# A transformer block with expert-choice routing on one core: routing's second search by two bits a round, its first list on four engines, an add moved behind a gather, and constants made later

## The chip, the cores and the metric

The kernel runs on one core of a Trainium2 chip. The metric is the device time of one execution in microseconds (us). A core has five engines that run their own instruction streams and meet at semaphores: PE (TensorE, matmuls and transposes), DVE (VectorE), ACT (ScalarE), POOL (GpSimd) and SP (SyncE, which here issues DMAs). A profile's PEld rows are PE's loads of the stationary operand.

## The reference

The input is `x`, 16 sequences of 256 tokens of width 256 (4096 tokens in all), and one condition vector for each sequence. Everything is float32. Cut to what matters:

```python
shift = silu(t) @ W_ada.T + b_ada
h = ln(x, ln1_g, ln1_b) + shift
q, k, v = (h @ Wqkv.T)                 # 16 heads of 64
q, k = ln(q, qn_g, qn_b), ln(k, kn_g, kn_b)
o = softmax(q @ k.T / 8) @ v
x = x + o @ Wout.T
tok = x.reshape(4096, 256)
gate = softmax(tok @ Wgate.T)          # 8 experts
vals, idx = top_k(gate.T, 512)         # each expert picks its 512 best tokens
g = ln(tok[idx], mlp_g, mlp_b)
y = (gelu(g @ fc1.T + b1) @ fc2.T + b2) * vals
tok[idx] += y                          # scatter-add of all experts
```

## The kernel before

**Attention.** The 16 sequences follow each other, and neighbours overlap. For each sequence the kernel normalises x, projects it in six groups of 512 columns (q, k and v, L611), normalises q and k by head (square on ACT L624, sum on DVE L628, power on POOL L82, scale on DVE L644), transposes them, and takes the heads in quads: scores (L686), row maxima on DVE (L693), exponentials on ACT (L702), normalisation on POOL (L713), transposes on PE (L722), the product with v (L740). The output projection (L764) gives the tokens. They are written to `out`, and, normalised, to a table `xn_dram` that the experts gather from.

**Head.** Before the first projection the kernel loads x of sequence 0, the projection's weights and small tables, and takes the head mean out of the q and k weights ("centering", L531 to L533, eight times). POOL also makes the constants of routing there: block and triangle masks, lane numbers, tile numbers (L85 to L131).

**Routing.** Each of the 8 experts chooses 512 tokens in two halves of 256: the first 256 from the tokens of the first 15 sequences, the second 256 from all tokens that are left. For each half the gates stand as 128 rows of 256 (16 rows for each expert), and a binary search over the 30 bits of a float32 gate finds the value that 256 tokens reach. A round compares all gates with a candidate on DVE (`compare`, L881, with a count for each row), sums the 16 rows of each expert by a matmul on PE (first search `count_over` L911 and L912, second `count` L888), and takes or drops the bit on DVE (`decide` L927, or `drop` and `step`, L893 and L900). Then masks, running sums and offsets give each chosen token its place from 1 to 256 (`masks`, `totals`, `place`), PE turns the places so that tokens lie on partitions (`turn_places`, L967), and `split` makes two numbers of each place: the chunk of 128 and the place in it.

**Jobs.** There are 16 jobs, one for each half and expert. A job needs a list of its token numbers and weights. DVE builds a one-hot of the place for each of 30 or 32 token tiles (`onehot`, L1031) and the values to send there, masked by chunk (`gives`, L1013 and L1021), and PE adds up 30 or 32 small matmuls (`list_matmul`, L1040). `take` reads token numbers and weights from the sum, `gather` fetches the rows by two indirect DMAs on POOL's queue (L1059), PE transposes them (L1068), and two matrix products with GELU between follow (`up` L1087, `gelu` L1094, `down` L1103). `finish` adds the bias and multiplies by the weight on DVE (L1109, L1110), and `scatter` adds the 128 rows to `out` by an indirect DMA on POOL's queue (L1113). Each add waits until the add before it has landed, as both write `out`.

**What sets the order.** Nothing is scheduled by a program at run time: each engine executes its instructions in the order in which the code emits them. Up to job 0 the order comes from a hand-written table: every step has a number (`SEARCH`, `PLACE`, `LIST`, `UP`, `DOWN` and so on), all steps are sorted by it, and emitted. Steps of sequence b in the middle are shifted by `b * PERIOD`. In the table the one-hots of job 0's tiles 25 to 29 stand ahead of tiles 10 to 14; both fives are on POOL, the other twenty on DVE.

From job 1 on a loop emits 16 slots for each job: eight with two matmul pairs of `up`, eight with two of `down`. Into the slots it puts the steps of the second routing, one entry a slot (`second_routing`), the list of the next job (slot 5; in job 7, slot 7), its transposes (slot 14), and the one-hots of the job after it (slots 7 to 15 and 0 to 4). A round of the second search took three slots for the first nineteen bits and two for the last eleven:

```python
new = [partial(b.compare, 29)]
for n in range(29, -1, -1):
    yield from (new, [])
    if n > 10:
        yield []
    new = [partial(f, n) for f in (b.count, b.drop, b.step)]
    new.append(partial(b.compare, n - 1) if n else b.masks)
```

## Time and profile before

| | |
|---|---|
| Median of 3 runs | 1195.77 us (1191.63 to 1196.15) |
| The profiled execution | 1194.45 us, of which the span from first to last instruction is 1192.6 us |
| Mean granted clock of PE | 0.992 |
| Busy share of the span | PE 98%, PEld 69%, DVE 64%, ACT 52%, POOL 50% |
| First matmul, first projection | 5.08 us, 9.02 us |
| First search, first to last count on PE | 867.9 to 909.1 us |
| First list's matmuls | 920.1 to 923.7 us |
| Job 2's gathered rows are transposed | from 963.77 us |
| Second search, first to last count | 958.3 to 1038.7 us |
| Last matmul starts | 1182.4 us |

A line of the timeline gives the start and the length in us, the engine, the line of the kernel, the operation, what it writes and reads, the shapes, how many equal instructions were merged, and in brackets how long the engine was idle before it and what ended that. A letter q after an engine means its queue, issuing a DMA. A line of the waits names who waited for what, the total in us, how often, and the longest. The table by stretches gives for each stretch of time the busy time of each engine.

### The profile page before, as it was taken

Reading aid. Unit: us, or ns where it says so; the run is one execution under the profiler, and the core shown is the slowest. Engines: PE = TensorE matmul, PEld = TensorE weight load, DVE = VectorE, ACT = ScalarE, POOL = GpSimd, SP = SyncE. Lnnn points to the kernel's source line nnn. Section 1 sums busy time; section 2 is a strip of 40 time slices with the busy share of each in tenths; the row PEclk is TensorE's granted clock in tenths of the full one; section 3 lists DMA queues with packets and bytes.
Section 4 is the critical chain, followed back from the end, with each engine's and each line's share of the span. In section 5 each row is a group of like instructions: output and inputs, shape, how many; then the busy total and the mean of one; then the engine's idle time right before and its main releaser. Section 6 shows DMA issues by size and latency. Waiting matters only on the chain. (4 is left out here: it accounts for less than half of the span.)

```text
span 1192.6 us, 19612 instructions
## 1 busy us (share of the span) xinstructions
PE 1162.9 (98%) x6814; PEld 817.1 (69%) x6814; DVE 760.9 (64%) x2274; ACT 624.5 (52%) x1701; POOL 590.7 (50%) x820
## 2 busy tenths in 40 slices
PE   7999999999999999999999999999998989999996
PEld 3566666666676666666666666667755878888885
DVE  7665576666566666666666666565588557865541
ACT  2765655565565656565656566556574422333331
POOL 4665455545555555555554555464674233333332
PEclk9999999999999999999999999999999999999999
DMA  5000000000000000000000000000200446666661
GB/s 187 1 1 5 14 18 19 10 18 10 19 23 5 23 10 19 10 23 6 23 10 28 9 11 14 14 19 19 85 9 1 168 129 186 186 186 185 183 185 22
DMA packets 46738, 62.40 MB, mean 52 GB/s; under 512 B 3888, under 2 KB 39984, under 8 KB 46640
## 3 DMA queue, kind: packets, MB, share of 16 engines
q1 hardware_dynamic: 37680, 49.82, 12.3%
q0 software_dynamic: 6144, 8.39, 3.8%
q10 hardware_dynamic: 2816, 2.95, 0.7%
q8 instruction: 54, 0.88, 0.3%
q14 instruction: 44, 0.36, 0.1%
HBM read 48.56 MB, written 12.58 MB: 51 GB/s over the span
## 5 line engine op out<-in xcount | busy, mean ns | idle before, releaser
L611 PE MATMUL pm<-wq,hT 128*128 128x512 f32 x768 | 365.3, 606 | 2.2 <-ACT qT L665 0.9
L713 POOL TENSOR_SCALAR pr<-pr,sums 128x256 f32<-128x256 f32 x512 | 236.8, 481 | 208.9 <-DVE sums L709 162.2
L82 POOL TENSOR_TENSOR ss<-ss,neghalf 128x8 f32<-128x8 f32 x128 | 211.5, 1653 | 189.8 <-DVE ss L632 185.4
L702 ACT ACTIVATE pr<-sc,nmax 128x256 f32<-128x256 f32 x512 | 236.1, 474 | 116.1 <-DVE nmax L693 111.1
L611 PEld LDWEIGHTS pm<-wq,hT 128*128 128x128 f32 x768 | 134.9, 192 | 126.3 <-issue 112.2
L693 DVE TENSOR_REDUCE nmax<-sc 128x2 f32<-128x512 f32 x256 | 166.5, 683 | 38.3 <-PE sc L686 38.1
L628 DVE TENSOR_REDUCE ss<-sq 128x8 f32<-128x512 f32 x128 | 87.3, 682 | 112.0 <-ACT sq L624 111.5
L722 PEld LDWEIGHTS pp<-ident,pr 128*128 128x128 f32 x1024 | 119.1, 142 | 43.6 <-POOL pr L713 20.3
L722 PE MATMUL pp<-ident,pr 128*128 128x128 f32 x1024 | 139.2, 273 | 0.2
L624 ACT ACTIVATE sq<-pm 128x512 f32<-128x512 f32 x128 | 76.7, 600 | 113.6 <-PE pm L611 107.1
L686 PE MATMUL sc<-kT,qT 64*128 64x256 f32 x1024 | 129.2, 390 | 0.0
L740 PE MATMUL po<-prT,v 128*64 128x256 f32 x1024 | 126.7, 389 | 0.0
L686 PEld LDWEIGHTS sc<-kT,qT 64*128 64x128 f32 x1024 | 93.2, 186 | 40.6 <-issue 30.4
L1103 PE MATMUL py<-w,hid 128*128 128x256 f32 x512 | 118.8, 385 | 0.0
L1087 PE MATMUL ph<-xT,w 128*128 128x256 f32 x512 | 118.4, 384 | 0.0
L764 PE MATMUL pw<-wo,oT 128*128 128x256 f32 x512 | 118.0, 384 | 0.0
L1113 POOL DMA_INDIRECT out<-y,idx x32 | 51.6, 1611 | 123.9 <-DVE y L1110 72.9
L764 PEld LDWEIGHTS pw<-wo,oT 128*128 128x128 f32 x512 | 96.8, 192 | 18.9 <-issue 6.5
L1094 ACT ACTIVATE hid<-ph,vec 128x256 f32<-128x256 f32 x128 | 60.3, 473 | 85.5 <-PE ph L1087 73.4
L1103 PEld LDWEIGHTS py<-w,hid 128*128 128x128 f32 x512 | 95.8, 192 | 13.4
L702 ACT ACTIVATION_READ_ACCUMULATOR pr<-sc,nmax 128x1 f32 x512 | 104.9, 205 | 0.0
L1087 PEld LDWEIGHTS ph<-xT,w 128*128 128x128 f32 x512 | 95.3, 191 | 13.4
(129 smaller groups left out, 1290.7 us busy)
## 6 DMA issues: line engine op xcount, KB each, us to landing
w<-in_fc2T SPq DMA_DIRECT2D x16, 1024.0 KB, 5.6
w<-in_fc1T SPq DMA_DIRECT2D x16, 1024.0 KB, 8.0
out<-tok SPq DMA_DIRECT2D x32, 128.0 KB, 1.7
xn_dram<-tn SPq DMA_DIRECT2D x32, 128.0 KB, 1.7
xs<-in_x SPq DMA_DIRECT2D x15, 256.0 KB, 2.7
b<-in_b2s SPq DMA_DIRECT2D x16, 128.0 KB, 8.2
wq<-in_wqkvT SPq DMA_DIRECT2D x3, 512.0 KB, 6.6
wq<-in_wqkvT ACTq DMA_DIRECT2D x3, 512.0 KB, 6.6
```

Of the source, the lines that this page charges most:

```text
L82: nc.gpsimd.tensor_tensor(dst, src, neghalf[:, : src.shape[1]], ALU.pow)
L611: nc.tensor.matmul(self.pm, hTs[self.b][:, c, bass.ts(self.t, P)], wq[:, c, bass.ts(self.g, GW)], start=(c == 0), stop=(c == DC - 1),)
L628: nc.vector.tensor_reduce(self.ss[:, 0, :], self.sq.rearrange("p (h d) -> p h d", d=HD), AX.X, ALU.add,)
L686: nc.tensor.matmul(self.sc[i, j][:, t, :], qTs[self.b][rows, hp, bass.ts(t, P)], kTs[self.b][rows, hp, :], start=True, stop=True,)
L693: nc.vector.tensor_reduce(self.nmax[i, j], self.sc[i, j], AX.X, ALU.max, negate=True)
L702: nc.scalar.activation(self.pr[i, j][:, t, :], self.sc[i, j][:, t, :], AF.Exp, bias=self.nmax[i, j][:, t : t + 1], scale=1.0, accum_out=se ...
L713: nc.gpsimd.tensor_scalar(self.pr[i, j][:, t, :], self.pr[i, j][:, t, :], self.sums[i][:, 1, j, t : t + 1], 1.0, ALU.mult, ALU.mult,)
L722: nc.tensor.transpose(self.pp[i, j][:, c, bass.ts(t, P)], self.pr[i, j][:, t, bass.ts(c, P)], ident,)
L740: nc.tensor.matmul(self.po[j * HD : (j + 1) * HD, i, :], vs[self.b][:, c, bass.ts(4 * self.d + 2 * i + j, HD)], self.prT[i, j][:, c, :], s ...
L764: nc.tensor.matmul(self.pw, oTs[self.b][:, hp, bass.ts(self.t, P)], wo[:, hp, :], start=(hp == 0), stop=(hp == HP - 1),)
L1087: nc.tensor.matmul(self.ph[f], self.w1[:, c, bass.ts(f, P)], self.xT[:, c, :], start=(c == 0), stop=(c == DC - 1),)
L1103: nc.tensor.matmul(self.py[i], self.hid[:, f, bass.ts(i, P)], self.w2[:, f, :], start=(f == 0), stop=(f == FC - 1),)
```

## The change

- **Constants.** Those of routing leave the head. Six steps placed at `(4 + k/8) * PERIOD` make them in sequence 4. `less` goes; `lane1` (lane numbers from 1), `begin` (−255 in every 16th row, else 0) and the tile numbers times 128 are new. The scaled q gain is made when the first shift is.
- **Head.** The condition is loaded ahead of the vectors. Centering is two operations instead of three. x of sequences 2, 3 and 4 is loaded from ACT's queue, with the output weights, by `last_loads`, behind the first q; before, SP's queue issued them.
- **First search.** The comparison starts its count from `begin`; the second matmul of each round, of one row and one column, goes.
- **Places.** The running sums start from 0 ahead of the offsets; two fused operations add the offset and mask. The turn adds the two kinds of place in PSUM by four matmuls. `split` works on the result in float32.
- **Lists.** `gives` is a product and a difference; for job 0 they run on POOL. The ten one-hots that were on POOL are twenty activations on ACT: `1 - |place - lane|`, clipped at 0. `take` reads the sum in PSUM directly.
- **Second search.** A round tests three candidates and settles two bits: 15 rounds of five slots.
- **Jobs.** `weigh` multiplies the bias by the weight ahead of time, and `finish` is one operation. Job 0's second `scatter` is emitted after the gather of job 2.

`fill` is defined but `FILL` is empty, so it emits nothing. The diff, cut to its core:

```diff
+    def make_vals(k):
+        nc.gpsimd.iota(
+            vals[:, :, :, k], pattern=[[0, E], [P * (1 - k), NT]], base=0, channel_multiplier=k,
+            allow_small_or_imprecise_dtypes=True,
+        )
+    def make_others():
+        nc.gpsimd.memset(gate_of, -1.0)
+        nc.gpsimd.memset(high, 1 << 29)
+        nc.gpsimd.iota(first16, pattern=[[0, 1]], base=0, channel_multiplier=1)
+        nc.vector.tensor_scalar(first16, first16, 15, None, ALU.bitwise_and)
+        nc.vector.tensor_scalar(begin, first16, 0.0, float(1 - CAPL), ALU.is_equal, ALU.mult)
...
+    LOADS = (-61.203, -19.863)
...
-            for g in (1, 3, 5):
+            for g in (5, 1, 3):
                 load_wq(g, nc.scalar)
+        def last_loads():
+            load_x(2, nc.scalar)
             nc.scalar.dma_start(wo, woutT.rearrange("(h p) d -> p h d", p=P))
+            for b in (3, 4):
+                load_x(b, nc.scalar)
...
-            nc.vector.tensor_scalar_mul(ws, ws, 1.0 / HD)
-            nc.vector.tensor_tensor(
-                w3, w3, ws.unsqueeze(2).to_broadcast([P, 8, HD]), ALU.subtract
+            nc.vector.scalar_tensor_tensor(
+                w3, ws.unsqueeze(2).to_broadcast([P, 8, HD]), -1.0 / HD, w3, ALU.mult, ALU.add
...
-                    reach, self.gT, self.cand.bitcast(F32), None, ALU.is_ge, ALU.add,
+                    reach, self.gT, self.cand.bitcast(F32), start, ALU.is_ge, ALU.add,
...
+            def candidates(self, n):
+                self.three = bit.tile([P, 3], I32, tag="three", name="three")
+                for k in range(3):
+                    new = self.three[:, k : k + 1]
+                    if n == 28:
+                        nc.vector.memset(new, (k + 1) << n)
+                    else:
+                        nc.vector.tensor_scalar(
+                            new, self.cand, (k + 1) << n, 0, ALU.bitwise_or, ALU.bitwise_or
+                        )
+            def compare_three(self, n):
+                self.cnt = bit.tile([P, 3], BF16, tag="cnt3", name="cnt3")
+                for k in range(3):
+                    reach = bit.tile([P, 2 * P], BF16, tag="reach", name="reach")
+                    nc.vector.tensor_scalar(
+                        reach, self.gT, self.three[:, k : k + 1].bitcast(F32), None,
+                        ALU.is_ge, ALU.add, accum_out=self.cnt[:, k : k + 1],
+                    )
+            def count_three(self, n):
+                self.pc = ps.tile([P, 3], F32, tag="mm", bufs=3, name="pc")
+                nc.tensor.matmul(self.pc, block, self.cnt, start=True, stop=True)
+            def choose_bits(self, n):
+                enough = bit.tile([P, 3], F32, tag="enough", name="enough")
+                many = bit.tile([P, 1], F32, tag="many", name="many")
+                nc.vector.tensor_scalar(
+                    enough, self.pc, CAPL - 0.5, None, ALU.is_ge, ALU.add, accum_out=many
+                )
+                bits = bit.tile([P, 1], I32, tag="bits", name="bits")
+                nc.vector.tensor_scalar(bits, many, float(1 << n), None, ALU.mult)
+                if n == 28:
+                    self.cand = bits
+                else:
+                    old, self.cand = self.cand, bit.tile([P, 1], I32, tag="cand", name="cand")
+                    nc.vector.tensor_tensor(self.cand, old, bits, ALU.bitwise_or)
...
+                self.compare(n, begin)
...
-                nc.tensor.matmul(self.pc, ones[:1, :P], less, start=True, stop=False)
-                nc.tensor.matmul(self.pc, twice, self.cnt, start=False, stop=True)
+                nc.tensor.matmul(self.pc, twice, self.cnt, start=True, stop=True)
...
-                    offset[:, 1:2], offset[:, 2:3], offset[:, 1:2], ALU.add
...
+            def scans(self):
+                self.place_ = route.tile([P, 2, 2 * P], F32, tag="place", name="place")
                 for m in range(2):
                     nc.vector.tensor_tensor_scan(
-                        place[:, m], ones, self.mask[:, m], offset[:, m : m + 1],
-                        ALU.mult, ALU.add,
-                    )
-                nc.vector.tensor_tensor(place, place, self.mask, ALU.mult)
-                nc.vector.tensor_tensor(place[:, 0], place[:, 0], place[:, 1], ALU.add)
-                self.places = place[:, 0]
+                        self.place_[:, m], ones, self.mask[:, m], 0.0, ALU.mult, ALU.add
+                    )
+            def totals(self):
+                self.po = ps.tile([P, 2], F32, tag="mm", bufs=3, name="po")
+                nc.tensor.matmul(self.po[:, :1], below, self.tot[:, :1], start=True, stop=True)
+                nc.tensor.matmul(self.po[:, 1:], below, self.tot[:, 1:], start=True, stop=False)
+                nc.tensor.matmul(self.po[:, 1:], block, self.tot[:, :1], start=False, stop=True)
+            def place(self):
+                offset = route.tile([P, 2], F32, tag="offset", name="offset")
+                nc.vector.tensor_copy(offset, self.po)
+                for m in range(2):
+                    nc.vector.scalar_tensor_tensor(
+                        self.place_[:, m], self.place_[:, m], offset[:, m : m + 1],
+                        self.mask[:, m], ALU.add, ALU.mult,
+                    )
...
-                    nc.tensor.transpose(
-                        self.pp[:, r, :], self.places[:, bass.ts(r, P)], ident
-                    )
+                    for m in range(2):
+                        nc.tensor.matmul(
+                            self.pp[:, r, :], self.place_[:, m, bass.ts(r, P)], ident,
+                            start=(m == 0), stop=(m == 1),
+                        )
...
+                chunk, place = (
+                    self.part[:, k].rearrange("p (k r) -> p r k", r=2) for k in range(2)
+                )
+                nc.vector.tensor_scalar(chunk, self.pp, P + 0.5, None, ALU.is_gt)
+                nc.vector.scalar_tensor_tensor(
+                    place, chunk, -float(P), self.pp, ALU.mult, ALU.add
+                )
...
-            def gives(self):
+            def gives(self, engine=nc.vector):
                 e, n = self.e, self.tiles
-                chunk = moe.tile([P, NT, KL], BF16, tag="chunk", name="chunk")
-                nc.vector.tensor_tensor(
-                    chunk[:, :n],
+                self.give = moe.tile([P, NT, KL, NV], BF16, tag="give", name="give")
+                engine.tensor_tensor(
+                    self.give[:, :n, 1, :], vals[:, e, :n],
                     self.routing.part[:, 0, e * NT : e * NT + n]
-                    .unsqueeze(2).to_broadcast([P, n, KL]),
-                    lane[:, :KL].unsqueeze(1).to_broadcast([P, n, KL]), ALU.is_equal,
-                )
-                self.give = moe.tile([P, NT, KL, NV], BF16, tag="give", name="give")
-                for c in range(KL):
-                    nc.vector.tensor_tensor(
-                        self.give[:, :n, c, :], vals[:, e, :n],
-                        chunk[:, :n, c : c + 1].to_broadcast([P, n, NV]), ALU.mult,
-                    )
+                    .unsqueeze(2).to_broadcast([P, n, NV]), ALU.mult,
+                )
+                engine.tensor_tensor(
+                    self.give[:, :n, 0, :], vals[:, e, :n], self.give[:, :n, 1, :], ALU.subtract
+                )
...
-                    engine.tensor_scalar(
-                        self.oh[:, t, :], lane, self.routing.part[:, 1, k : k + 1], None,
-                        ALU.is_equal,
-                    )
+                    place = self.routing.part[:, 1, k : k + 1]
+                    if engine is nc.scalar:
+                        off = moe.tile([P, P], BF16, tag="off", name="off")
+                        nc.scalar.activation(off, lane1, AF.Abs, bias=place, scale=-1.0)
+                        nc.scalar.activation(self.oh[:, t, :], off, AF.Relu, bias=1.0, scale=-1.0)
+                    else:
+                        nc.vector.tensor_scalar(
+                            self.oh[:, t, :], lane1, place, None, ALU.is_equal
+                        )
...
+                with nc.allow_low_precision(reason="whole numbers below 2 ** 12"):
+                    nc.vector.tensor_reduce(self.idx, self.pls[:, :, :2], AX.X, ALU.add)
                 self.w = moe.tile([P, KL], F32, tag="w", bufs=4, name="w")
-                nc.vector.tensor_reduce(self.w, ls[:, :, 2:], AX.X, ALU.add)
+                nc.vector.tensor_reduce(self.w, self.pls[:, :, 2:], AX.X, ALU.add)
...
+            def weigh(self):
+                self.bw = moe.tile([P, KL, D], F32, tag="bw", name="bw")
+                for i in range(KL):
+                    nc.vector.tensor_scalar_mul(self.bw[:, i], self.b2, self.w[:, i : i + 1])
             def finish(self, i):
-                nc.vector.tensor_tensor(self.y[:, i], self.py[i], self.b2, ALU.add)
-                nc.vector.tensor_scalar_mul(self.y[:, i], self.y[:, i], self.w[:, i : i + 1])
+                nc.vector.scalar_tensor_tensor(
+                    self.y[:, i], self.py[i], self.w[:, i : i + 1], self.bw[:, i],
+                    ALU.mult, ALU.add,
+                )
...
+        for k, f in enumerate((
+            make_block, make_twice, make_lanes, partial(make_vals, 0), partial(make_vals, 1),
+            make_others,
+        )):
+            at([(4 + k / 8) * PERIOD], f)
...
-            at([p["gives"]], a.gives)
+            at([p["gives"]], partial(a.gives, nc.gpsimd if a is jobs[0] else nc.vector))
...
-                engine = nc.gpsimd if a is jobs[0] and k in (2, 5) else nc.vector
+                engine = nc.scalar if a is jobs[0] and k in (2, 5) else nc.vector
...
-            at(DOWN[i][1:], partial(jobs[0].scatter, i))
+        at([UP[0][0]], jobs[0].weigh)
+        by_end = sorted(range(KL), key=lambda i: DOWN[i])
+        at(DOWN[by_end[0]][1:], partial(jobs[0].scatter, by_end[0]))
...
+            new = [partial(f, 28) for f in (b.candidates, b.compare_three)]
+            for n in range(28, -1, -2):
+                yield from (new, [], [], [], [])
+                new = [partial(f, n) for f in (b.count_three, b.choose_bits)]
+                new += [partial(f, n - 2) for f in (b.candidates, b.compare_three)] if n else [b.masks, b.scans]
...
                     new.list_matmul(0, NT)
                     new.take()
                     new.gather()
+                    if k == 1:
+                        jobs[0].scatter(by_end[1])
...
+                    if s == FC - 1:
+                        a.weigh()
```

## The prediction

> **What bounds the kernel now.** I read the page first, then busy time and granted clock by stretch, the matrix engine's waits, and the timeline of the stretches where it waits.
>
> ```profile
> PE 1162.9 (98%) x6814; PEld 817.1 (69%) x6814; DVE 760.9 (64%) x2274; ACT 624.5 (52%) x1701; POOL 590.7 (50%) x820
> ...
> PE   7999999999999999999999999999998989999996
> ```
>
> PE is busy from end to end: work taken off another engine is worth only what PE waits for it. Counting each PE instruction at its undisturbed spacing in the trace (429 ns for 512 columns, 216 for 256, 109 for a 128-column transpose), I get 1083 us of a 1192.6 us span. Of the rest, about 35 us is spread evenly over the sixteen sequences. What can be moved lies at the head (first matmul at 5.08, then about 11 us lost before 40) and from 875 to 969.
>
> ```profile
> 910.00:914.00 4.00, 3.75 (x21) 1.83 (x19) 3.21 (x10) 0.58 (x1) 0.57 (x2) 0.61 0.01 4
> ...
> 920.00:924.00 4.00, 1.95 (x34) 1.38 (x32) 2.67 (x15) 0.00 (x0) 3.22 (x5) 1.00 0.00 0
> 924.00:928.00 4.00, 4.00 (x12) 3.23 (x11) 3.93 (x25) 0.00 (x0) 2.22 (x2) 0.57 0.21 53
> ...
> 961.00:965.00 4.00, 0.55 (x4) 0.19 (x2) 1.60 (x9) 0.00 (x0) 3.38 (x3) 1.00 0.23 68
> 965.00:969.00 4.00, 4.00 (x13) 3.26 (x14) 0.20 (x1) 1.02 (x2) 0.00 (x0) 0.57 0.30 35
> ```
>
> Columns: length, then busy us of PE, PEld, DVE, ACT, POOL, granted clock, DMA share, GB/s. PE stands still at 920 and 961, and each standstill is paid again: the clock of the next 4 us is 0.57, and there a 256-column matmul takes 0.42 instead of 0.216 us.
>
> ```profile
> PE pc L912 <- DVE reach L881: 4.0, 14, 0.5
> PE px L1068 <- DMA xg<-xn_dram,idx: 3.8, 3, 2.6
> PE pls L1040 <- POOL oh L1031: 1.9, 4, 0.5
> ```
>
> From 850 to 975 these three waits lead: the first search, the gather of job 2, and the one-hots of the first list on POOL.
>
> **1. Second add of job 0 behind a gather: −5.4.**
>
> ```profile
> 949.07 1.67 POOL L1113 DMA_INDIRECT out<-y,idx  x1 [11.43 <-DVE y L1110]
> ...
> 957.61 1.57 POOL L1113 DMA_INDIRECT out<-y,idx  x1 [6.87 <-DMA out<-y,idx]
> ...
> 960.71 1.05 POOL L1059 DMA_INDIRECT xg<-xn_dram,idx  x1
> ...
> 962.06 0.99 POOL L1059 DMA_INDIRECT xg<-xn_dram,idx  x1 [0.30 <-issue]
> ```
>
> The second add waits 6.87 us for the first to land (956.83), and behind it in POOL's queue stand the gates' parts (five operations, 2.0 us) and both gathers of job 2, whose indices have been there since 953.38. PE came for the gathered rows at 961.06 and lost 2.74 + 1.07 us, then about 1.6 to the slow clock. Moved, the gathers are issued at about 953.5 and 954.8. What is late next is their landing: POOL's queue of transfers still holds the first add until 956.83, and the gathers of 934.30 and 935.55, behind weight loads too, took until 939.7 and 940.0. Both give a landing at 957.5 to 959.5, 2 us or more before PE comes. The moved add now waits behind the gathers; who waits for it is only the next job's add, whose y is ready at 960.5. Bounds −3.5 to −6.
>
> **2. First list over four engines: +2.1, a loss.** PE turns the places at 914.65, when DVE had been done since 913.6: the shorter chain before (scans ahead of the totals) is covered by PE. The turn becomes four accumulating float32 matmuls instead of two transposes. A float32 matmul leaves two records (L1103: two of 216 for 256 columns), so 4 × 2 × 109 = 0.87 instead of 0.22 us: +0.65. The split falls from 1.41 (four operations to 916.48) to about 0.88 (two of 0.42 plus gaps), so parts are ready at 916.6, as before. The two "gives" go to POOL: its 128x16 subtraction takes 0.22, the 128x224 one 0.70, so about 0.54 each for 150 columns, 1.1 in all, done by 917.8; PE comes at 920.7, so this is hidden. Gone from POOL are ten one-hots, 6.65 us from 916.57 to 923.22, the wait above. In their place ScalarE does twenty activations of 128 columns, and in its queue they stand behind the last copy of the attention's output:
>
> ```profile
> 916.57 6.65 POOL L1031 TENSOR_SCALAR oh<-lane,partf 128x128 bf16<-128x128 bf16 x10 [6.00 <-DVE partf L981]
> ...
> 917.52 0.58 ACT L750 COPY oT<-po 128x512 f32<-128x512 f32 x1 [2.03 <-PE po L740]
> ```
>
> That copy ends at 918.10, or 918.75 with PE later by 0.65. No 128-column activation is in the trace. The 16-column one lasts 0.21, the 256-column one 0.473 (0.356 from start to start): 0.335 between, the second of each pair reading the first. 20 × 0.335 = 6.7, end 925.45; then 15 list matmuls of 25 ns: PE leaves at 925.85 instead of 923.70. Tiles 25 to 29 are made ahead of 10 to 14, so PE needs the very last. The Trainium skill (ScalarE: Activation LUTs, "Rules for kernel authors") speaks against this step: such cheap functions belong on VectorE, and an activation costs about 0.3 us plus 0.83 ns per element, 0.41 here: by that the twenty take 8.1 us and the loss is 3.6. With half of each pair overlapped (0.335 + 0.24) it is 5.75, loss 1.2. I take the rows. Job 0's gather and VectorE's one-hots of job 1 shift with PE; the slow stretch after it is there already.
>
> **3. First search: −0.6.** Thirty matmuls of 1x1 go. Where PE goes on at once (14 steps) one costs 0.105: −1.5. In the 16 others PE then waits 0.3 to 0.6 for `reach`; the loop of comparison, count and decision (1.05 us) sets the step, and nothing is saved. The comparison gets a second per-partition scalar: the f32 128x256 operation with two (L553, 0.405) lasts 0.05 more than that with one (L1110, 0.353). In 16 waiting steps that is at most +0.9. Bounds −1.5 to 0.
>
> **4. Second search in pairs of bits: +1.3.** PE waited for it nowhere: each count takes 0.03 us of PE and DVE waits for PE (8.8 us, L893). So fewer rounds buy 15 × 0.03 = −0.45, and the second turn of places costs +0.65. DVE pays. Before: 30 × 0.86 (drop 0.19, step 0.20, comparison 0.40 plus its 0.085). Now per round: `enough` with its accumulator 0.25, bits and candidate 0.2 each, three candidates 0.29 (0.15 and two more at 0.065), three comparisons 3 × 0.41 + 0.08: 2.3, × 15 = 34 instead of 26. A job has 16 slots of 0.864 plus list, transposes and counts: 15.1 us. DVE then holds 3.2 rounds 7.4, 30 one-hots at 0.166 5.0, gives 0.6, take 0.3, weighing 0.7, finish 0.9: 14.9. Full, but not over, and lumpy. Worst is job 7's list in slot 5 of job 6: two slots earlier the last choice (0.65), masks (0.9) and now both scans (1.4) run in one piece, then the last three one-hots: 0.2 + 2.95 + 0.5 = 3.65 after the slot began, when PE would be through at 1.73 + 0.75: +1.1. Small waits at two other lists +0.3; job 8's list, which waited 0.28, gains 0.3. Bounds 0 to +6 (rival B).
>
> **5. Head: −1.2.**
>
> ```profile
> 3.40 0.83 POOL L112 IOTA vals<- 128x256 bf16 x1
> 3.71 1.51 DVE L123 TENSOR_SCALAR qgb<-vec 128x2 f32<-128x2 f32 x1 [3.71 <-DMA vec<-in_vecs]
> 3.90 1.33 DVE L543 BATCH_NORM_STATS2 st<-xs 128x6 f32<-128x256 f32 x1
> 4.00 0.94 POOL L116 IOTA vals<- 128x256 bf16 x1
> ```
>
> DVE's two-column operation lasts 1.51 us and ends at 5.22, just as POOL's run of constants ends (5.20); the statistics queued behind it take 1.33 instead of 0.42. Both go: −0.9 on the way to the first projection (9.02), whose weights landed at 7.52. Eight centerings lose an operation of 0.2 us; one is on the path (the scale at 21.21 queues behind it), another less so: −0.3. x of sequences 2 to 4 moves from SP to ScalarE's queue, four issues of 0.4 to 0.7 at about 23 us, where ScalarE is idle for 3.7 us; without that cover it would be 2.0 late. Bounds 0 and −2.5 (the 0.64 clock of 24 to 28 gone too).
>
> **6. Constants in sequence 4: +0.2.** Thirteen POOL operations (4.9 us) at six places. Three fall into idle of 1.7 to 6 us; the others delay POOL by 0.82, 0.66 and 0.65. Normalised scores are ready at least 0.9 us before PE turns them there. VectorE's two operations on `first16` wait for POOL at the last place, with a reciprocal behind them, which POOL itself needs. The skill (SBUF — State Buffer, "SBUF: two separate sides") says that a GpSimd operation and a two-port VectorE one exclude each other; the head's 1.5 us shows such a hold, but only under a run of constants; here each run is under 0.9 us and DVE is busy 64%. By the rule taken at its worst six holds would cost 4 us of DVE, which has it. Bounds 0 and +2.
>
> **7. End: −0.4.** The last finish is one operation instead of two (0.42 + 0.04 + 0.35), and the scatters follow. Of the earlier ones PE waits for none.
>
> Sum: −5.4 + 2.1 − 0.6 + 1.3 − 1.2 + 0.2 − 0.4 = −4.0. The profiled execution took 1194.45 us (span 1192.6): 1190.4. It lies 1.3 below the median of the runs, 1195.77, so I give 1191.8.
>
> **Rivals.**
> A, ScalarE is quick and the head gains in full (20 × 0.29, and the cold clock at 24 gone): list +1.2, head −2.5, search −1.5: −7.2, 1188.6. For it: activations start every 0.356 at 256 columns. Against: the pairs depend. 23%.
> B, slower: VectorE becomes the bound in the second search. If small operations do not overlap (three candidates at 0.19, comparisons at 0.49), a round is 2.7 and a job 16.2 us, over 15.1; it decides from 2.35 us a round. Five jobs × 1.1 in place of small waits: +6 in place of 1.3, so +0.7 in all; with the list at 8.1 us, +2.2: 1198.0. For it: 14.9 of 15.1. Against: candidates overlap now (0.065 apart). 17%.
> C, the reordered gather lands late behind the first add and weight loads, and half of the stall stays: −1.5 instead of −5.4: 1195.7. For it: such a gather took up to 5.4 us to land. Against: 2 us of slack. 18%.
> The sum: 42%.
>
> Within 0.5%, 6 us, is about what a measurement can tell from no change. All of A and a quarter of the likeliest lie below 1189.8: faster 33%. Over 1201.7 only the end of B: 6%. The range reaches from A's far side to near B: 1185.5 to 1197.5; the likeliest case's own is 1189 to 1194.5.
>
> **What would show it.** Right: no wait on job 2's gather and clock 1.0 after it; PE's wait in the first list on ScalarE, not POOL, and longer; first statistics about 0.45 us; job 7's list waits for VectorE. Wrong: PE waiting at most lists of jobs 3 to 7 (B), a first list leaving sooner than before relative to the turn of places (step 2), or sequence 4 longer than its neighbours by over 1 us (step 6).

## The result and the profile after

| | before | after |
|---|---|---|
| Median of 20 runs | 1194.57 us (1191.24 to 1196.17) | 1189.94 us (1187.09 to 1194.47) |
| Ratio of the two | | 0.9968, interval 0.9957 to 0.9979 |
| The profiled execution, its span | 1194.45, 1192.6 us | 1189.26, 1187.5 us |

By the ratio the kernel became about 3.8 us faster (0.32%, interval 0.21 to 0.43%); the medians alone differ by 4.6. The time lies inside the range given and near its likeliest value. The two profiles differ by 5.1 us of span. The sections below show why that is more than the ratio gives, and that the sum came out right with several of its terms wrong.

The page after, busy time and tenths of PE:

```profile
PE 1155.4 (97%) x6783; PEld 814.6 (69%) x6783; DVE 758.9 (64%) x2303; ACT 630.4 (53%) x1721; POOL 585.5 (49%) x813
...
PE   7999999999999999999999999999987999999996
```

PE still bounds the kernel. What PE waits for between 850 and 975 us (line, what it waited for, us in total, times, longest):

```profile
PE pc L956 <- DVE reach L901: 7.1, 16, 0.8
PE pls L1091 <- ACT oh L1081: 3.3, 5, 1.5
PE px L1116 <- DMA xg<-xn_dram,idx: 1.8, 2, 1.3
PE pc L956 <- DVE drop L962: 1.2, 1, 1.2
```

The search's wait has doubled, the first list waits for ScalarE and not POOL, and a wait for gathered rows is still there. But that is another gather: job 1's, at 937, where before only 0.3 us were lost. The stretches (columns as in the prediction: length, busy us of PE, PEld, DVE, ACT, POOL, granted clock, DMA share, GB/s):

```profile
910.00:914.00 4.00, 4.00 (x35) 2.67 (x32) 2.44 (x10) 1.24 (x3) 0.90 (x2) 1.00 0.00 0
916.00:920.00 4.00, 1.45 (x17) 0.93 (x15) 1.86 (x11) 3.78 (x14) 0.00 (x0) 0.96 0.00 0
920.00:924.00 4.00, 3.28 (x23) 2.72 (x24) 2.46 (x16) 0.82 (x3) 1.69 (x2) 0.50 0.03 6
...
940.00:944.00 4.00, 4.00 (x13) 3.18 (x12) 0.00 (x0) 1.02 (x2) 0.00 (x0) 0.57 0.00 0
961.00:965.00 4.00, 4.00 (x23) 3.45 (x22) 3.59 (x23) 1.02 (x2) 1.36 (x1) 1.00 0.32 35
```

The standstill at 961 and the slow clock after it are gone. New are the standstill at 916 to 920, where ACT is busy all the time, and slow stretches at 920 and 940. At 910, where before had a clock of 0.61, the clock is now full, though nothing in the change asks for that. POOL's queue after (start, length, what ended the idle time before):

```profile
950.29 1.67 POOL L1168 DMA_INDIRECT out<-y,idx  x1 [14.30 <-DVE gates L844]
...
954.61 1.03 POOL L1107 DMA_INDIRECT xg<-xn_dram,idx  x1 [0.54 <-DVE idx L1100]
955.94 0.96 POOL L1107 DMA_INDIRECT xg<-xn_dram,idx  x1 [0.30 <-issue]
958.92 1.63 POOL L1168 DMA_INDIRECT out<-y,idx  x1 [2.03 <-DMA out<-y,idx]
...
971.21 1.55 POOL L1168 DMA_INDIRECT out<-y,idx  x1 [5.95 <-DVE give L1068]
973.07 1.01 POOL L1107 DMA_INDIRECT xg<-xn_dram,idx  x1 [0.30 <-DVE reach L922]
```

The gathers of job 2 now stand ahead of the second add of job 0 (958.92). At 971.21 the second add of job 1 still stands ahead of the gather of job 3 (973.07): the same pattern, one job later.

To see where the profiles part, I take the start of the same PE work in both (before, after, difference):

| PE starts | before | after | difference |
|---|---|---|---|
| first projection | 9.02 | 8.45 | −0.56 |
| projection of sequence 1 | 46.35 | 43.51 | −2.84 |
| projections of sequences 2 to 15 | | | −2.84 or −2.85 each |
| first count, last count of the first search | 867.86, 909.07 | 864.93, 907.00 | −2.93, −2.07 |
| first list, first and last matmul | 920.10, 923.67 | 916.51, 921.33 | −3.60, −2.34 |
| transposes of job 1 | 939.73 | 938.68 | −1.05 |
| list of job 2 | 952.08 | 953.24 | +1.16 |
| transposes of job 3 | 982.24 | 977.61 | −4.63 |
| list of job 7, last matmul | 1036.87 | 1032.05 | −4.83 |
| transposes of job 9 | 1075.79 | 1071.11 | −4.68 |
| last matmul; span | 1182.39; 1192.65 | 1177.72; 1187.54 | −4.68; −5.11 |

Read alone, this says: head −2.8 (−2.9 by the first count), search +0.9, first list and what follows +1.0 (places −1.5, list +1.3, slow clock and the rest +1.3), job 1's gather and the slow clock behind it +2.2, job 2's gather −5.8, second search 0, end −0.4. Two of these, the head and the places, are mostly not the change's doing, as the experiments show.

### The profile page after: what moved, and what is told of

It is laid out like the page before. It is cut to its first block, busy times and chain, and to the rows that moved or that the text cites. A ratio compares the mean times of both kernels' runs of the same rounds, so it can differ in the third digit from the quotient of the medians.

```text
span 1187.5 us, 19592 instructions
## 1 busy us (share of the span) xinstructions
PE 1155.4 (97%) x6783; PEld 814.6 (69%) x6783; DVE 758.9 (64%) x2303; ACT 630.4 (53%) x1721; POOL 585.5 (49%) x813
## 3 DMA queue, kind: packets, MB, share of 16 engines
q1 hardware_dynamic: 36864, 49.03, 12.4%
```

## The experiments

Times are medians; ratios are to the kernel before, and the changed kernel's own is 0.9968. A difference to the changed kernel is that of the ratios times 1194.57 us. The changed kernel was not run again beside the experiments, and each ratio has an interval of 0.0011 to 0.0018 to either side, so a difference to it of less than about 2 us may be nothing.

**1. The moved add put back.**

```diff
-        at(DOWN[by_end[0]][1:], partial(jobs[0].scatter, by_end[0]))
+        for i in by_end:
+            at(DOWN[i][1:], partial(jobs[0].scatter, i))
...
-                    if k == 1:
-                        jobs[0].scatter(by_end[1])
```

> The changed kernel with one thing undone: job 0's second add is emitted ahead of job 2's gather again. Theory (place in POOL's queue): the gathers of job 2 are issued only after the first add has landed; PE's wait at job 2's transposes comes back with 2.5 to 4 us, and a stretch at half clock after it; in all 5.2 to 5.9 us longer than the changed kernel, so at or above the kernel before (ratio to it 1.000 to 1.002). Rival (the gathers land sooner because the weight loads lie elsewhere, the place in the queue is worth half at most): 0 to 2.8 us longer than the changed kernel, ratio 0.997 to 0.999.

1197.57 us, ratio 1.0030 (1.0015 to 1.0044): 7.4 us more than the changed kernel. The gather's waits are back (the 6.4 us hold job 1's 2.0 and 0.1, and job 2's 3.5 and 0.9):

```profile
PE px L1116 <- DMA xg<-xn_dram,idx: 6.4, 3, 3.5
```

From the list of job 2 to the transposes of job 3 the profile takes 6.5 us longer than that of the changed kernel (30.1 instead of 23.6, from the start of the list's last matmul). The theory holds. And the rest of the change, without this part, makes the kernel slower than before.

**2. The moved add alone,** in the kernel before.

```diff
-            at(DOWN[i][1:], partial(jobs[0].scatter, i))
+        by_end = sorted(range(KL), key=lambda i: DOWN[i])
+        at(DOWN[by_end[0]][1:], partial(jobs[0].scatter, by_end[0]))
...
                     new.gather()
+                    if k == 1:
+                        jobs[0].scatter(by_end[1])
```

> The kernel before with one part of the change: job 0's second add behind job 2's gather. Theory: PE's wait at job 2's transposes (3.4 us and the half-clock stretch behind it, 5.9 us in all) goes, 1 to 2 us come back at job 3's transposes in some executions: 3.5 to 6 us below the kernel before, ratio 0.995 to 0.997, so more than the whole change gives. Rival (the part has its worth only together with the other parts): under 3 us, ratio over 0.9975.

1187.87 us, ratio 0.9938 (0.9924 to 0.9952): 7.4 us faster than before, and about 3.6 us faster than the whole change. Its waits from 850 to 985:

```profile
PE pc L912 <- DVE reach L881: 4.0, 14, 0.5
PE pls L1040 <- POOL oh L1031: 2.8, 5, 0.7
...
PE px L1068 <- DMA xg<-xn_dram,idx: 0.3, 1, 0.3
```

The search and the list wait about as in the kernel before, and of 3.8 us for gathered rows 0.3 are left. In the profile the stretch from job 2's list to job 3's transposes shrinks by 5.5 us. The two experiments agree: the part is worth 5.5 to 6.5 us by the traces and 7.4 by the times (5.7 to 9.1 in the second), and the other parts together cost 3.6.

**3. Five one-hots on ScalarE instead of ten.**

```diff
-                engine = nc.scalar if a is jobs[0] and k in (2, 5) else nc.vector
+                engine = nc.scalar if a is jobs[0] and k == 5 else nc.vector
```

> The changed kernel with five of the first list's one-hots on ScalarE instead of ten (tiles 25 to 29); VectorE makes 25. Theory (ten pairs of activations at 0.63 us each set the end of the first list, and the standstill puts the clock to one half after it): VectorE has its 25 by 917.3, ScalarE its five by 917.7; PE leaves the list at about 918 instead of 921.3, so 3.3 us sooner, and up to 2.2 us more if no stretch at half clock follows; the wait at job 1's gathered rows stays as it is, because its weights start when PE's last output projection ends and so move along. In all 3 to 5.5 us shorter than the changed kernel (ratio to the kernel before 0.992 to 0.995). Rival (job 1's gather lands at its own time, whatever the list does): the gain passes into a longer wait at job 1's transposes, 0 to 1 us in all.

1185.91 us, ratio 0.9932 (0.9914 to 0.9950): 4.3 us below the changed kernel. PE leaves the list at 918.24, 1.2 us after it came, as against 4.8, and the profile has no half-clock stretch from 12.4 us to the end of PE's work. The wait at job 1's transposes fell to 0.1 us. But at job 3's transposes 1.6 us of waiting appeared, and POOL's queue says why:

```profile
966.33 1.56 POOL L1168 DMA_INDIRECT out<-y,idx  x1 [8.10 <-DVE reach L922]
968.20 1.01 POOL L1107 DMA_INDIRECT xg<-xn_dram,idx  x1 [0.30 <-issue]
969.52 0.97 POOL L1107 DMA_INDIRECT xg<-xn_dram,idx  x1 [0.30 <-issue]
```

Job 1's first add, issued at 956.65 just ahead of job 3's weights, landed at 965.59, when the weights were nearly in; the second add could go only then, and the gather stood behind it, though its list had left PE at 962.17. The first-list part of the theory holds; that the waits behind it would stay as they were does not.

**4. Job 1's second weight block from ScalarE's queue,** behind the fourth GELU of job 0.

```diff
-                self.w2 = seq.tile([P, FC, D], F32, tag="oT", name="w2")
-                nc.sync.dma_start(self.w2, fc2T[e].rearrange("(f p) d -> p f d", p=P))
+                if self is not jobs[1]:
+                    self.load_w2(nc.sync)
...
+        at([UP[1][1] + 0.001], partial(jobs[1].load_w2, nc.scalar))
```

> The changed kernel with the second weight block of job 1 (1 MB) issued from ScalarE's queue behind the fourth GELU of job 0, so after job 1's gathers instead of ahead of them. Theory (job 1's gathered rows wait behind 2 MB of weights in the DMA engines): the rows land 2 us sooner or more, PE's waits of 1.3 and 0.5 us at job 1's transposes and the half-clock stretch after them (1.5 us) go: 2.2 to 3.6 us shorter than the changed kernel (ratio to the kernel before 0.993 to 0.995). Rival (the gather itself takes over 5 us from issue to landing, whatever is loaded beside it): no change within 0.5 us, or longer because the weights come late for job 1's second product.

1192.40 us, ratio 0.9987 (0.9974 to 0.9999): 2.3 us above the changed kernel, where 2 to 4 below were expected. The profile:

```profile
933.66 1.15 POOL L1111 DMA_INDIRECT xg<-xn_dram,idx  x1 [6.82 <-DVE idx L1104]
...
934.84 0.38 ACTq L1061 DMA_DIRECT2D w<-in_fc2T  x1
935.11 0.95 POOL L1111 DMA_INDIRECT xg<-xn_dram,idx  x1 [0.30 <-issue]
...
940.64 0.55 PE L1120 MATMUL px<-ident,xg 128*128 128x128 f32 x3 [1.88 <-DMA xg<-xn_dram,idx]
```

The first gather, issued before the block, landed after 3.2 us (936.89), and PE did not wait for it. The second, issued 0.3 us after the block, landed at 940.59, just after the block (940.24). So rows do queue behind weights, but I had put the block one gather too early.

**5. The same, behind the sixth GELU.**

```diff
-        at([UP[1][1] + 0.001], partial(jobs[1].load_w2, nc.scalar))
+        at([UP[3][1] + 0.001], partial(jobs[1].load_w2, nc.scalar))
```

> The changed kernel with the second weight block of job 1 issued from ScalarE's queue behind the sixth GELU of job 0, so behind both of job 1's gathers (two GELUs later than in the earlier try, where the second gather was issued 0.3 us after the block and landed behind it). Theory: both gathers land within 3.5 us of their issue, PE waits under 0.3 us in all at job 1's transposes and no half-clock stretch follows at 940; list 2 starts 2.2 to 3.6 us sooner than in the changed kernel. Rival (the gathers are slow by themselves): the second wait stays at over 1 us.

1189.63 us, ratio 0.9963 (0.9948 to 0.9977). All four transposes of job 1 now run without a wait:

```profile
940.18 0.63 PE L1120 MATMUL px<-ident,xg 128*128 128x128 f32 x4
```

From the end of job 1's list to the start of job 2's the profile takes 19.7 us; the changed kernel took 23.6, experiment 1 22.2, the kernel before 20.9. The mechanism is shown. Its worth in the times is not: 0.6 us below the changed kernel, no difference at this width of interval, and experiment 4, with part of the wait left, was even above. Why so little of the 2.5 us between 22.2 and 19.7 arrives stays open.

**6. POOL's constants in the head again.**

```diff
+    make_block()
+    make_twice()
+    make_lanes()
+    make_vals(0)
+    make_vals(1)
...
-            make_block, make_twice, make_lanes, partial(make_vals, 0), partial(make_vals, 1),
             make_others,
```

> The changed kernel with routing's constants (block, below, ones, lanes, tile numbers) made by POOL in the head again; the condition's load, the two-operation centering and the loads of x stay as in the change. Theory (POOL's run of constants holds VectorE's first statistics): the first statistics take over 1 us instead of 0.42, the first projection starts 0.4 to 0.9 us later, and the whole is 0.4 to 0.9 us longer than the changed kernel; whether a stretch at half clock follows at 20 to 27 us depends on where the 3.4 us stretches of the clock lie in that execution and is the same for both. Rival (the hold came from the scaled gain, which waited for its vectors on VectorE): no change at the first projection, within 0.2 us.

1191.62 us, ratio 0.9988 (0.9976 to 1.0000). The first projection came 0.15 us later instead of 0.4 to 0.9, so the theory fell. POOL's long run of iotas, and beside it the first statistics:

```profile
3.56 1.54 POOL L121 IOTA vals<- 128x256 bf16 x2
3.92 0.43 DVE L568 BATCH_NORM_STATS2 st<-xs 128x6 f32<-128x256 f32 x1 [3.92 <-DMA xs<-in_x]
```

The statistics take 0.43 us under the same run of constants where they took 1.33, and the first projection starts at 8.60, against 8.45. Constants alone held nothing. (By the ratios it is 2.4 us above the changed kernel; 1.6 us of its profile are a wait at job 3's transposes like that of experiment 3.)

**7. Most of the old head:** also the scaled gain, ahead of the statistics in the program, and centering in three operations.

```diff
...
+    nc.vector.tensor_scalar_mul(qgb, vec[:, QN_G : QN_B + 1], HD**-0.5)
...
-            nc.vector.scalar_tensor_tensor(
-                w3, ws.unsqueeze(2).to_broadcast([P, 8, HD]), -1.0 / HD, w3, ALU.mult, ALU.add
-            )
+            nc.vector.tensor_scalar_mul(ws, ws, 1.0 / HD)
+            nc.vector.tensor_tensor(
+                w3, w3, ws.unsqueeze(2).to_broadcast([P, 8, HD]), ALU.subtract
+            )
```

> The changed kernel with most of the old head: the scaled q gain and POOL's constants ahead of the first statistics, and centering in three operations; the order of the first loads stays new. Theory (the hold needs both POOL's constants and VectorE's gain beside them, as constants alone held nothing): the gain takes over 1 us, the first statistics start after it, the first projection starts 0.5 us later than in the changed kernel; with three-operation centering the first scores' transposes are 0.8 to 1.5 us later if no half-clock stretch comes, up to 3 us if one does. Rival (the whole gain of the head was where the clock's stretches lay in the one execution): the projection of sequence 1 starts within 0.6 us of the changed kernel's profiles without such a stretch (43.4 to 44.2 us).

1191.96 us, ratio 0.9978 (0.9965 to 0.9990). The first projection starts at 8.71, that of sequence 1 at 46.71. The gain beside POOL's constants, and the gain in the changed kernel, where POOL has no constants to make:

```profile
3.57 1.54 POOL L121 IOTA vals<- 128x256 bf16 x2
...
4.63 0.51 DVE L139 TENSOR_SCALAR qgb<-vec 128x2 f32<-128x2 f32 x1 [0.48 <-DMA vec<-in_vecs]
```

```profile
6.54 0.16 DVE L520 TENSOR_SCALAR qgb<-vec 128x2 f32<-128x2 f32 x1
```

The gain takes 0.51 us here and not 1.5, as it got its vectors only at 4.63; but it ends at 5.14, just when POOL's constants end (5.11). In three profiles with the old head (before, before again, experiment 2) it starts at 3.46 to 3.77 and ends each time at 5.22 or 5.23, and POOL's run ends at 5.20. So the old hold is there, only shorter: the gain lasts until POOL's run ends, and what stands behind it on VectorE waits. Experiment 6, which had POOL's run without the gain under it, held nothing. By the ratios the old head costs 1.2 us, less than the intervals can tell from nothing. Sequence 1 starts 0.4 us later than in experiment 1 and 0.7 later than in experiment 5, which have the new head.

**8. The kernel before once more.** By now eight profiles held the unchanged new head, and sequence 1 started at 43.4 to 44.2 us in six of them and at 46.0 and 46.3 in two.

> The kernel before, unchanged, profiled once more. Theory (where the 3.4 us stretches of the clock lie against the kernel's start differs between executions and decides most of the head's difference between the two first profiles): if the clock is first full before 12.6 us, the projection of sequence 1 starts at 43.7 to 45.0 us, within 1 us of the changed kernel's profiles of that kind (43.4 to 44.2), and no half-clock stretch lies at 23 to 28; if it is first full later, at 46 to 47.5 us, as in the first profile (46.35). Rival (the old head is slower by itself): 46 us or more in either case.

One execution: 1191.43 us, span 1189.5, so 3.1 us shorter than the first profile of the same kernel. Sequence 1 starts at 44.44 instead of 46.35. The stretch from 24 us in the first profile of before, in this one, and in experiment 5 with the new head:

```profile
24.00:28.00 4.00, 4.00 (x13) 1.91 (x13) 3.83 (x10) 0.81 (x2) 0.41 (x1) 0.64 0.00 0
```

```profile
24.00:28.00 4.00, 4.00 (x18) 2.10 (x17) 3.83 (x10) 2.09 (x4) 0.03 (x1) 1.00 0.00 0
```

```profile
24.00:28.00 4.00, 4.00 (x12) 2.11 (x12) 3.86 (x9) 1.25 (x2) 0.06 (x1) 0.61 1.04 345
```

The granted clock is 0.64, 1.00 and 0.61: the old head can have a full clock there, and the new one a slow one. The times show it too: of the 29 runs of the kernel before that stand beside experiment 1, every one above 1194.2 us has a mean granted clock of 0.992, and every one below it 0.993 to 0.995. The trace's record of the clock gives the half-clock stretches to the nanosecond. Up to PE's last matmul each is 3.413 us long, or twice that, and within one execution their starts lie a multiple of 3.413 us apart (first profile of before: 23.45, 910.91, 924.56, 965.52). From one execution to the next this grid lies elsewhere against the kernel's start. Where the clock was first full at 11.5 to 12.5 us, no slow stretch followed in the head, in either kernel; where it was first full at 13.2 to 14.0, one followed at 23.4 to 24.2, in either kernel. (In experiment 2 it was first full only at 17.04; no slow stretch followed in the head, and sequence 1 started at 47.28.) The Trainium skill (TensorE: Matmul & The Clock Gate, "What's actually happening") says that the clock is set by a window of 3413 ns that runs free and does not restart with the kernel; the traces agree to the digit.

**9. The second search by single bits again,** the rest as changed.

```diff
-            new = [partial(f, 28) for f in (b.candidates, b.compare_three)]
-            for n in range(28, -1, -2):
-                yield from (new, [], [], [], [])
+            new = [partial(b.compare, 29)]
+            for n in range(29, -1, -1):
+                yield from (new, [])
+                if n > 10:
+                    yield []
...
```

> The changed kernel with the second search by single bits again (30 rounds in slots of three and two, as before); the rest of the change stays. Theory (PE waits for the second search in neither form, so that the pairs of bits save only what fifteen counts cost PE, and cost one wait at job 7's list): from list 3 to job 9's transposes 0 to 0.7 us longer or shorter than the changed kernel, VectorE less busy there, ratio to the changed kernel 0.999 to 1.001. Rival (VectorE full to 14.9 of 15.1 us a job is what makes job 7's list wait and jobs late): PE's wait at job 7's list falls from 0.5 us to nothing and the stretch is over 1 us shorter.

1192.91 us, ratio 0.9988 (0.9977 to 0.9999). That is 2.4 us above the changed kernel. From list 3 to job 9's transposes the profile takes 103.5 us, against 102.3: 1.2 more, of which 0.4 is a wait for job 3's rows. The wait at job 7's list is indeed gone, but the stretch is longer, not shorter. By this profile pairs of bits are a small gain, and the rival falls.

**10. Job 1's second add behind job 3's gather.**

```diff
                     if k == 1:
                         jobs[0].scatter(by_end[1])
+                    if k == 2:
+                        jobs[1].scatter(1)
...
-                        a.scatter(i)
+                        if (k, i) != (1, 1):
+                            a.scatter(i)
```

> The changed kernel, and the second add of job 1 is emitted behind the gather of job 3 as well. Theory (the moved add of job 0 lands at 963, pushes job 1's first add into the weight loads of job 3, where it takes 7 us to land, so that job 3's gathers stand in POOL's queue behind job 1's second add, and land in some executions after PE has come): the gathers of job 3 are issued right after its list (at about 970 instead of 973), no execution waits at job 3's transposes, where two of four profiles waited 2 us; median 0.5 to 2 us below the changed kernel. Rival (the wait there comes from the weight loads of job 3 alone): job 3's rows land no sooner, no change in the median.

1189.78 us, ratio 0.9964 (0.9949 to 0.9980). The gathers of job 3 are issued at 969.82 and 971.14, 3.3 us sooner, and PE does not wait. Mechanism as expected, worth in the median unclear (0.5 us): in the changed kernel's own profile the rows were just in time.

**11. Experiments 3, 5 and 10 together.**

> The changed kernel with three edits: five of the first list's one-hots on ScalarE instead of ten, the second weight block of job 1 issued from ScalarE's queue behind the sixth GELU of job 0 (behind both gathers of job 1), and job 1's second add behind job 3's gather. Theory: PE waits neither at the first list (under 0.8 us) nor at the transposes of jobs 1, 2 and 3 (under 0.5 us in all, beside those of job 0), 5 to 7 us below the changed kernel, ratio to the kernel before 0.990 to 0.993. Rival (the time before a job's transposes is fixed by how fast the weights land, and an edit only moves the wait from one job to the next): 4 us below the changed kernel, as with the one-hots alone.

1184.68 us, ratio 0.9906 (0.9891 to 0.9921): 7.4 us below the changed kernel, a little more than expected. For gathered rows PE waits once from 850 to 985, at job 0:

```profile
PE px L1120 <- DMA xg<-xn_dram,idx: 0.5, 1, 0.5
```

**12. The same, with the 1x1 matmul back in the first search and sixteen dummy transposes first.**

```diff
-                self.compare(n, begin)
+                self.compare(n)
...
-                nc.tensor.matmul(self.pc, twice, self.cnt, start=True, stop=True)
+                nc.tensor.matmul(self.pc, ones[:1, :P], less, start=True, stop=False)
+                nc.tensor.matmul(self.pc, twice, self.cnt, start=False, stop=True)
...
-    FILL = ()
+    FILL = (16,)
```

> The three edits of the best version so far (five one-hots on ScalarE, job 1's second weight block behind its gathers, job 1's second add behind job 3's gather), and two more: the 1x1 matmul in the first search again instead of the second scalar of the comparison, and sixteen transposes of the identity ahead of PE's first work, which nothing reads. Theory: the loop of the first search is bound by VectorE's comparison, which is 0.06 us quicker with one scalar: from the first count to the last 41.2 us as in the kernel before instead of 42.07; the dummy transposes keep PE busy from 1.5 to 5 us, so that the clock is full 3 us sooner and the projection of sequence 1 starts 0.5 to 2 us sooner (at 41.8 to 43.3). In all 1 to 3 us below the version with three edits. Rival for the search (the 1x1 matmul's 0.1 us of PE is what counts): first to last count 42 us or more. Rival for the head (centering on VectorE sets when the projections can go on, not the clock): sequence 1 starts within 0.3 us of 43.8.

1182.49 us, ratio 0.9898 (0.9883 to 0.9912), the fastest version run, if not separable from the eleventh. From first to last count 41.21 us, as in the kernel before (the changed kernel: 42.07), with the old wait:

```profile
PE pc L960 <- DVE reach L904: 4.0, 14, 0.5
```

So the search's theory holds for the two edits together; that it is the second scalar that costs is read from the comparison's 537 and 477 ns, shown below. In the one profile the dummy transposes did nothing for the clock: PE was busy from 1.44 us, yet the clock was first full at 13.26, and sequence 1 started at 46.28.

## Why the prediction was right, and where it was not

The forecast of −4.0 met a measured −3.8 by the ratio, but through terms that cancel: the first step, the one that decides the sign, was right in mechanism, and the closeness of the sum was largely luck. To weigh the terms at a nearly equal clock I compare experiment 1 with the first profile of before, whose clocks are first full at 13.75 and 13.21 and which have the same slow stretches at 24, 911 and 925. That gives the change without its first step: span +3.4 us, by the times +3.6. The whole change at a nearly equal clock is seen in the changed kernel's profile and the second one of before (first full at 11.75 and 12.46): there it is worth 2.0 us of span, and not 5.1.

| Step | forecast | measured |
|---|---|---|
| 1, second add behind a gather | −5.4 | −5.5 and −6.5 in traces, −7.4 in times |
| 2, first list over four engines | +2.1 | +0.2 up to its first matmul, +1.25 within it, −0.4 behind it |
| 2, job 1's gather behind the list | not forecast | +1.2 |
| 3, first search | −0.6 | +0.86 |
| between job 1's and job 3's transposes, with the add ahead (step 1's stall) | not forecast | +0.8 |
| 4, second search | +1.3 | −0.05 |
| 5, head | −1.2 | 0 to −0.6 at an equal clock |
| 6, constants in sequence 4 | +0.2 | 0.0 |
| 7, end | −0.4 | −0.3 |

**Step 1** was right in mechanism; the size was at or beyond its upper bound of 6. (The prediction's 2.74 and 1.07 us of lost time are 2.57 and 0.88 of PE itself; the 3.8 of the waits hold 0.3 at job 1's transposes.) The stall is longer in experiment 1, 3.5 and 0.9 us: PE came 13.2 us after the issue of job 2's first weight block in both, but the first add took 9.0 us to land, where it took 7.8 in the first profile of before. "Who waits for it is only the next job's add" was too short a look. The next add drops into job 3's weight loads (landed at 970.47 after 6.8 us, where before it took 3.9), and the gather of job 3 stands behind the add after that: of eight profiles with the moved add, and job 1's second add where the change left it, two waited 1.6 us there, three 0.3 to 0.4, three not at all. Rival C named weight loads, but at the wrong gather (and the 1.5 it left of 5.4 is less than the half it spoke of).

**Step 2**: PE's wait went from POOL to ScalarE and became longer, as said. Each pair of activations takes 0.63 us, within the bounds; the two operations:

```profile
L1080 ACT ACTIVATE off<-lane,partf 128x128 bf16<-128x128 bf16 x10 | 3.9, 388 | 0.0
L1081 ACT ACTIVATE oh<-off 128x128 bf16<-128x128 bf16 x10 | 3.1, 309 | 0.3
```

Together 0.70, of which 0.07 overlaps; my 0.67 for a pair was close. The price of the rule that the prediction quotes from the Trainium skill (ScalarE: Activation LUTs, "Rules for kernel authors"), 0.41 us each and 8.1 for the twenty, was too high: they took 6.45 (914.41 to 920.86). The rule's 0.3 us is given for an activation whose bias is a per-partition operand; only the first of each pair has one, and that one took 0.388. They started 3.5 us after PE began turning the places, where I had 4.1, so the list ended 10.4 us after that instead of 11.2 (before: 9.0). What the longer list costs depends on the clock too: from the last count to the list's last matmul it is 16.0 us in experiment 1 against 14.6 before, with a slow stretch at 911 in both, but 14.3 in the changed kernel against 13.7 and 13.9 in the second profile of before and in experiment 2, which have none there. Job 1's gather was not in the sum. Its rows queue behind 2 MB of weights whose load starts when PE's last output projection ends, and 0.3 us of waiting became 1.8 (2.1 in experiment 1), in the changed kernel's profile with a slow stretch behind it. Counted from the issue of the first of these blocks, PE came for the rows after 8.9 us in experiment 1, against 9.4 before; the second block landed after 10.0 us, against 8.2, and the rows after 10.8, against 9.7. So PE comes sooner, but the larger part is that weights and rows land later, and the cause of that stays open.

**Step 3** failed in its gain. A comparison with two scalars takes 537 ns, as against 477, so the 0.05 was right (0.06). After, then before:

```profile
L901 DVE TENSOR_SCALAR_CACHE_REDUCE reach<-gT,cand,begin 128x256 bf16<-128x256 f32 x29 | 15.6, 537 | 0.7
```

```profile
L881 DVE TENSOR_SCALAR_CACHE_REDUCE reach<-gT,cand 128x256 bf16<-128x256 f32 x29 | 13.8, 477 | 0.7
```

But the 0.105 us of the 1x1 matmul in the 14 steps "where PE goes on at once" was no saving: what PE no longer spends there, it waits for the comparison. Waits for `reach` and `drop` rose from 4.0 to 8.3 us, more than the roughly 3.1 us of matmuls that went. The loop on VectorE sets the pace: the measured +0.86 is the "at most +0.9" that the prediction gave its 16 waiting steps, with nothing saved in the 14 others.

**Step 4**: the piece on VectorE at job 7's list came as forecast,

```profile
1029.44 0.48 DVE L981 TENSOR_SCALAR_CACHE_REDUCE mask<-gT,cand 128x256 f32<-128x256 f32 x1
...
1030.24 1.27 DVE L989 TENSOR_TENSOR_SCAN place<-ones,mask 128x256 f32<-128x256 bf16 x2
1031.43 0.56 DVE L1083 TENSOR_SCALAR oh<-lane,partf 128x128 bf16<-128x128 bf16 x3
```

and cost 0.8 us instead of 1.1 (the last one-hots come after the scans, and PE for them). The counts saved 1.1 up to that list instead of 0.45: there were 13 fewer of them (26 and 13 between 969 and 1035), so each costs PE about 0.085, not 0.03, if they account for all of it. The waits at two other lists did not come. Rival B is refuted: between 969 and 1035 VectorE is busy 56.2 of 66 us and no other list waits.

**Step 5** is where the first profile misleads. It shows −2.84, beyond the bound of −2.5 that had the slow clock gone. At an equal clock the new head's sequence 1 starts at 46.0 and 46.3 beside the old one's 46.35, and at 43.8 to 44.0 (first full at 12.2 to 12.4) beside 44.44. The first projection did start 0.56 sooner, where 0.9 was forecast, but in the profile after, a weight load of PE then waits 0.69 us, until 11.34, for the centered weights. The hold itself is as the prediction read it, the gain under POOL's run with the statistics queued behind it; experiments 6 and 7 show that it takes both. What was mis-sized is what it is worth: at sequence 1, 0 to 0.6 us of the step's 1.2 are left. Rival A had "the cold clock at 24 gone" as an effect of the change; it is a matter of the execution.

**Steps 6 and 7** hold: sequence 4 takes 55.69 us in both kernels.

Of the signs named, all four for "right" came (no wait at job 2's gather with a full clock after it; a longer wait, for ScalarE; first statistics of 0.43 us; job 7's list waiting for VectorE), and none for "wrong". They did not look at job 1's and job 3's gathers, which is where the unforeseen microseconds were.

## What to carry to other kernels

When a transfer is moved ahead of a waiting one in a queue, follow the moved one to its landing and look who stands behind it there; the stall can come back one round later. An instruction taken off an engine that then waits for another's loop saves nothing, and whatever lengthens that loop costs in the rounds that wait for it. And before a difference of two profiles is put down to a change, look whether the stretch differs in the granted clock: the same kernel, profiled twice, differed by 3.1 us.

## What the runs showed of the hardware that was not expected

- The half-clock stretches lie on a grid of 3.413 us, whose place against the kernel's start differs between executions. Low use of PE in the 3.4 us before goes with a slow stretch (0.42, 0.54 and 0.26 busy before three of those in the first profile of before), but not as one threshold: 0.75 busy was followed by one at 910.91, and 0.60 by none in the changed kernel's search; 0.48 was followed by one at 940.17 in the changed kernel, and 0.48 from 962.66 on by none in experiment 1. What the gate counts stays open.
- Sixteen dummy transposes that kept PE busy from 1.44 to 5.1 us did not bring the full clock sooner (13.26).
- A gather of 128 rows took 2.8 to 3.0 us from the start of its issue to landing when no weights were under way (five of the 32 in the first profile of before, one from 960.71 to 963.63). The other 27 landed 0.7 to 2.9 us after the last weight block issued ahead of them.
- POOL's iotas (1.54 us for two) ran beside VectorE's statistics without slowing them (0.43 us), but the scaling of a two-column gain beside POOL's constants lasted until POOL's run ended: 1.45 to 1.77 us in three profiles and 0.51 in a fourth, against 0.16 with none beside it.
